# Explicit bounds and skipping in the row gathers of a recommendation kernel on Trainium2

## The chip, the cores and the metric

One core of one Trainium2 chip runs the whole kernel. The engines are named as in the profile: PE (TensorE matmul; PEld is its weight load), DVE (VectorE), ACT (ScalarE), POOL (GpSimd) and SP (SyncE); a trailing "q" (POOLq, SPq) means the engine's sequencer, which reads its instruction list and issues the work. The metric is device time in microseconds (us) of one execution, lower is better. The kernel before takes 32128.78 us, the median of three runs (32128.46 to 32131.62).

## The reference, cut to what matters

A click-through model with an attention over a user's history: 200 history positions (L) for each of 16384 users (B), embeddings of 64 float32 (D), tables of 100000 rows for users and items and 1000 rows for categories. Every history entry is a row fetched from the item table by its index.

```python
u, it, c, h = u_emb[user], i_emb[item], c_emb[cate], i_emb[hist]      # h: [200, 16384, 64]
itb  = broadcast(it, h.shape)
feat = concatenate([h, itb, h - itb, h * itb], axis=-1)
a    = dice(feat @ au_W1 + au_b1, au_alpha, axis=1)   # statistics over the 16384 users
w    = a @ au_W2 + au_b2
cur  = sum(w * h, axis=0)                             # over the 200 positions
z    = concatenate([u, it, c, cur], axis=-1)
z    = dice(z @ W1 + b1, alpha1, axis=0)
z    = dice(z @ W2 + b2, alpha2, axis=0)
out  = z @ W3 + b3
```

All indices given lie inside their tables (0 to 99999 for users and items, 0 to 999 for categories), so no row is ever out of bounds.

## The kernel before, in words

The 16384 users are cut into 128 tiles of 128 users (NT = 128). Sixteen tiles make a chunk, so a history position has 8 chunks (ND = 8, TD = 16). A step k handles one chunk of one position: 200 positions by 8 chunks are 1600 steps. Step k does work of several chunks at once: it fetches the rows of chunk k, transposes and multiplies chunk k - 1 (`turn`, `product`), measures chunk k - 2 (`hidden`, `measure`), and weighs chunk k - 10 into the running sums (`gate`, `weights`, `weigh`, LAG = 10).

Rows come in two ways. `fetch` (line 270) calls `gather` (line 116) once per tile; each call is one indirect DMA issued from POOL, which takes one index per partition out of `idx` and brings 128 rows of 256 bytes into one tile's place in `rows`. `rows` is a ring of five chunk buffers. The chunks 3 and 7 of every position have one tile less to gather (15 instead of 16): the rows of these two tiles are fetched one by one from SP by `rows_by_address` (line 254, its DMAs on line 265) into `side`, and ACT copies them into place. So a position needs 126 gathers, and 200 positions need 25200. Before the loop the same `gather` fetches the item rows (128 calls, line 398, indices from `ids[0]`), and after it the category and user rows (`head_fetch`, line 419, 128 calls each, indices from `ids[1]` and `ids[2]`).

The order on every engine is the order of the code, since all of it stands under a manual schedule; a hardware loop on line 406 runs 4 times over a body of 45 positions (line 408), and the last 20 positions are written out straight (line 441). POOL has nothing to do but gathers, apart from a handful of small instructions at the start. The DMA waits that the framework adds put the gathers on eight completion semaphores in turn, so a gather also waits for the one eight before it to have landed.

Of the kernel before, what the change touches and what calls it, by code (L numbers as in the profile page):

```python
# [32 lines left out]
def din_kernel(  # L33
# [82 lines left out]
    def gather(dst, ids, n, table):  # L116
        nc.gpsimd.indirect_dma_start(  # L117
            out=dst[:, n, :],
            out_offset=None,
            in_=table,  # L120
            in_offset=bass.IndirectOffsetOnAxis(ap=ids, axis=0),
        )

    def load_ids(t, v):
# [145 lines left out]
    def fetch(k):  # L270
        l, c = divmod(k, ND)
        for n in range(TD - has_side(k)):
            j = column(c, n)
            gather(rows[k % ROWS], idx[l % IDX][:, j : j + 1], n, i_emb)
# [98 lines left out]
    with tc.manual_schedule():  # L373
# [20 lines left out]
        for c in range(ND + 1):  # L394
            if c < ND:
                for n in range(TD):
                    j = column(c, n)
                    gather(rows[c % ROWS], ids[0][:, j : j + 1], n, i_emb)
            if c:
                transpose(itT[c - 1], rows[(c - 1) % ROWS])  # L400
# [18 lines left out]
    def head_fetch(k, j):  # L419
        c, u = divmod(j, 2)  # L420
        for n in range(TD):
            i = column(c, n)
            gather(rows[k % ROWS], ids[1 + u][:, i : i + 1], n, (c_emb, u_emb)[u])
# [128 lines left out]
```

## Time and profile before

The profile is of one execution.

| what | value |
|---|---|
| median of three runs | 32128.78 us |
| the profiled execution's own time | 32101.94 us |
| its span, first to last instruction | 32100.2 us |
| gathers from POOL | 25200 in the history steps, 3 x 128 around them |
| rows fetched one by one from SP | 51200 |
| busy share of DVE, the next busiest after POOL and PE | 46% |
| mean granted TensorE clock | 0.719 |

"Busy" counts an engine's own instructions; register, branch, semaphore and DMA-issuing instructions are not in it. "Idle before" is the time that an engine stood still ahead of an instruction, put down to what released it; "issue" as a releaser means that the engine waited for nothing that the profile shows. A line number is that of the instruction in the code above, so all gathers are L117, whichever loop called them.

### The profile page before, as it was taken

Reading aid. Unit: us, or ns where it says so; the run is one execution under the profiler, and the core shown is the slowest. Engines: PE = TensorE matmul, PEld = TensorE weight load, DVE = VectorE, ACT = ScalarE, POOL = GpSimd, SP = SyncE. Lnnn points to the kernel's source line nnn. Section 1 sums busy time; section 2 is a strip of 40 time slices with the busy share of each in tenths; the row PEclk is TensorE's granted clock in tenths of the full one; section 3 lists DMA queues with packets and bytes.
Section 4 is the critical chain, followed back from the end, with each engine's and each line's share of the span. In section 5 each row is a group of like instructions: output and inputs, shape, how many; then the busy total and the mean of one; then the engine's idle time right before and its main releaser. Section 6 shows DMA issues by size and latency. Waiting matters only on the chain. (4 is left out here: it accounts for less than half of the span.)

```text
span 32100.2 us, 224464 instructions
## 1 busy us (share of the span) xinstructions
PE 15661.4 (49%) x26020; PEld 6253.8 (19%) x26020; DVE 14921.9 (46%) x18956; ACT 7823.3 (24%) x7481; POOL 24139.4 (75%) x25589
## 2 busy tenths in 40 slices
PE   4444444444444444444445444454444444445445
PEld 1111121111111111111112111121111211112111
DVE  4444444444444444444444444444444444444443
ACT  2222222222222222222222222222222222222222
POOL 7777777777777777777777777777777777777776
PEclk7777767776777777777777777777777777777777
DMA  1111111111111111111111111111111111111111
GB/s 28 28 28 28 28 28 28 28 27 28 28 28 28 28 28 28 28 27 28 28 28 28 28 28 28 28 28 28 28 28 28 28 28 28 28 28 28 28 28 22
DMA packets 958596, 881.57 MB, mean 27 GB/s; under 512 B 547488, under 2 KB 547688, under 8 KB 957032
## 3 DMA queue, kind: packets, MB, share of 16 engines
q0 software_dynamic: 818688, 839.97, 11.8%
q1 hardware_dynamic: 138056, 27.05, 0.4%
q14 instruction: 1352, 11.08, 0.1%
q8 instruction: 212, 3.47, 0.0%
q10 hardware_dynamic: 288, 0.00, 0.0%
HBM read 865.03 MB, written 0.13 MB: 27 GB/s over the span
## 5 line engine op out<-in xcount | busy, mean ns | idle before, releaser
L117 POOL DMA_INDIRECT rows<-in_L_rec_i_emb,idx x25200 | 23776.6, 944 | 7706.1 <-issue 7132.8
L151 PE MATMUL px<-hT,blk_h 128*128 128x512 f32 x6404 | 5661.5, 983 | 15033.9 <-DVE hT L146 15033.9
L146 DVE STREAM_TRANSPOSE hT<-rows 64x512 f32<-64x512 f32 x6404 | 4519.1, 706 | 12085.3 <-DMA rows<-in_L_rec_i_emb,idx 11421.6
L304 ACT COPY ph<-hT 128x1024 f32<-128x1024 f32 x1601 | 1627.1, 1016 | 18738.7 <-DVE hT L146 18738.7
L151 PEld LDWEIGHTS px<-hT,blk_h 128*128 128x128 f32 x6404 | 1816.6, 314 | 18047.2 <-issue 17233.6
L151 PE MATMUL px<-itT,blk_i 128*128 128x512 f32 x6404 | 4735.4, 832 | 0.0
L151 PE MATMUL wb<-y,blk_w 128*128 128x512 f32 x6440 | 3413.4, 657 | 1245.9 <-DVE y L282 1230.2
L295 DVE BATCH_NORM_STATS2 st<-xs 128x6 f32<-128x512 f32 x3204 | 2058.3, 684 | 3704.4 <-ACT xs L290 3704.4
L151 PE MATMUL px<-hm,blk_m 128*128 128x512 f32 x6408 | 3036.9, 596 | 38.1 <-DVE hm L382 36.4
L290 ACT ACTIVATE xs<-px,au_bias 128x1024 f32<-128x1024 f32 x1602 | 1781.6, 1112 | 4164.1 <-PE px L151 4164.1
L151 PEld LDWEIGHTS px<-itT,blk_i 128*128 128x128 f32 x6404 | 1862.1, 291 | 2859.9 <-issue 2859.9
L282 DVE TENSOR_TENSOR y<-pg,xs 128x1024 f32<-128x1024 f32 x1610 | 1954.9, 1214 | 736.6 <-ACT pg L279 736.4
L286 DVE SCALAR_TENSOR_TENSOR wb<-wb,au_bias,hT 128x1024 f32<-128x1024 f32 x1610 | 2081.1, 1293 | 82.2 <-PE wb L151 30.0
L287 DVE TENSOR_TENSOR curT<-wb,curT 128x1024 f32<-128x1024 f32 x1610 | 1971.2, 1224 | 54.8
L278 ACT ACTIVATE pg<-xs,sh,rs 128x1024 f32<-128x1024 f32 x1610 | 1937.3, 1203 | 79.9 <-DVE sh L387 42.7
L307 DVE TENSOR_TENSOR hm<-ph,itT 128x1024 f32<-128x1024 f32 x1601 | 1942.5, 1213 | 0.0
L279 ACT ACTIVATE pg<-pg,au_al,au_1al 128x1024 f32<-128x1024 f32 x1610 | 1895.1, 1177 | 54.1
L151 PEld LDWEIGHTS wb<-y,blk_w 128*128 128x128 f32 x6440 | 1307.8, 207 | 2976.1 <-issue 1538.0
L151 PEld LDWEIGHTS px<-hm,blk_m 128*128 128x128 f32 x6408 | 1195.9, 191 | 1686.8 <-issue 1236.5
L278 ACT ACT_TABLE_LOAD x206 | 264.3, 1283 | 77.5 <-PEq L406 57.4
L160 ACT ACT_TABLE_LOAD x203 | 260.4, 1283 | 7.5 <-PE pg L461 4.0
L160 ACT ACTIVATE std<-var,eps 128x1 f32<-128x1 f32 x201 | 59.2, 294 | 710.6 <-DVE var L327 710.6
(147 smaller groups left out, 1531.7 us busy)
## 6 DMA issues: line engine op xcount, KB each, us to landing
side<-in_L_rec_i_emb SPq DMA_DIRECT2D x51200, 0.2 KB
rows<-in_L_rec_i_emb,idx POOLq DMA_INDIRECT x25200, 2.4
idx<-in_r_hist SPq DMA_DIRECT2D x200, 63.0 KB
addr<-in_r_hist SPq DMA_DIRECT2D x200, 1.0 KB
rows<-in_L_rec_i_emb,ids POOLq DMA_INDIRECT x128, 2.4
rows<-in_L_rec_c_emb,ids POOLq DMA_INDIRECT x128, 2.3
rows<-in_L_rec_u_emb,ids POOLq DMA_INDIRECT x128, 2.4
w1a<-in_L_rec_W SPq DMA_DIRECT2D x4, 32.0 KB
```

Of the source, the lines that this page charges most:

```text
L117: nc.gpsimd.indirect_dma_start(out=dst[:, n, :], out_offset=None, in_=table, in_offset=bass.IndirectOffsetOnAxis(ap=ids, axis=0),)
L146: nc.vector.transpose(by_tile(dst[ts(e, D)], i), of[ts(i, D), :, ts(e, S)])
L151: nc.tensor.matmul(dst[:, ts(i, CH)], lhsT, rhs[:, ts(i, CH)], start=(first and j == 0), stop=(last and j == len(pairs) - 1), skip_group_c ...
L278: nc.scalar.activation(pg, xs[k % XR], AF.Sigmoid, bias=shifts[i], scale=rstds[i])
L279: nc.scalar.activation(pg, pg, AF.Identity, bias=au_al, scale=au_1al)
L282: nc.vector.tensor_mul(y, pg, xs[k % XR])
L286: nc.vector.scalar_tensor_tensor(wb, wb, au_bias2, hT[k % LAG], ALU.add, ALU.mult)
L287: nc.vector.tensor_add(curT[k % ND], wb, curT[k % ND])
L290: nc.scalar.activation(xs[k % XR], px, AF.Identity, bias=au_bias)
L295: nc.vector.bn_stats(stats[l % 3][:, 2 * c + i, :], xs[k % XR][:, ts(i, CH)])
L304: nc.scalar.copy(ph, hT[k % LAG])
L307: nc.vector.tensor_mul(hm, ph, itT[k % ND])
```

## The change

Both arguments are added to the one call through which all gathers go:

```diff
             in_=table,
             in_offset=bass.IndirectOffsetOnAxis(ap=ids, axis=0),
+            bounds_check=table.shape[0] - 1,
+            oob_is_err=False,
         )
```

With `bounds_check` every index is compared with a bound (99999 for the user and item tables, 999 for the categories), and with `oob_is_err=False` a row whose index is greater is left out and nothing is reported. Without the two arguments the call gives no bound, and the instruction's flag says that an index out of bounds is an error.

In the built program the bound stands in a register of POOL's sequencer. The framework sets it anew ahead of every call: 8574 register moves are added to POOL's list, one ahead of each of the 8574 gathers in it (the loop body's 5670 are run four times). The gather instruction itself then names the register and has the error flag cleared; in the program before, the field of the register is empty and the flag is set. POOL's other instructions, their order and their waits are the same, and so are those of PE, DVE, ACT and SP.

## Prediction

> **What bounds the kernel now.** I read the page first, then the waits, then single instructions. The page's engines and costliest groups:
>
> ```profile
> PE 15661.4 (49%) x26020; PEld 6253.8 (19%) x26020; DVE 14921.9 (46%) x18956; ACT 7823.3 (24%) x7481; POOL 24139.4 (75%) x25589
> POOL 7777777777777777777777777777777777777776
> ...
> L117 POOL DMA_INDIRECT rows<-in_L_rec_i_emb,idx x25200 | 23776.6, 944 | 7706.1 <-issue 7132.8
> ```
>
> POOL looks 75% busy, evenly over the span, but the gather's idle time is not slack: 7706.1 us over 25200 gathers is 306 ns each, nearly all "issue". One gather takes 944 + 306 = 1249 ns from start to start, and 25,584 gathers (25,200 and three times 128) take 25,584 x 1.2493 = 31,962 us of the 32,100.2 us span. A stretch of the timeline confirms that the gap is the same every time (start and duration in us, idle time ahead):
>
> ```profile
> 15011.57 0.94 POOL L117 DMA_INDIRECT rows<-in_L_rec_i_emb,idx  x1 [0.30 <-issue]
> 15012.82 0.94 POOL L117 DMA_INDIRECT rows<-in_L_rec_i_emb,idx  x1 [0.30 <-issue]
> 15014.07 0.95 POOL L117 DMA_INDIRECT rows<-in_L_rec_i_emb,idx  x1 [0.30 <-issue]
> 15015.32 0.94 POOL L117 DMA_INDIRECT rows<-in_L_rec_i_emb,idx  x1 [0.30 <-DMA rows<-in_L_rec_i_emb,idx]
> ```
>
> The waits (in total, times, longest) say whether anyone holds POOL up, and who waits for it:
>
> ```profile
> PE px L151 <- DVE hT L146: 15033.9, 1596, 11.6
> DVE hT L146 <- DMA rows<-in_L_rec_i_emb,idx: 11421.6, 1498, 9.3
> POOL rows L117 <- issue: 7243.4, 23692, 8.0
> POOL rows L117 <- DMA rows<-in_L_rec_i_emb,idx: 533.7, 1750, 0.3
> ```
>
> The last row is no real wait: 533.7 / 1750 = 0.305 us, the ordinary gap. DVE waits 11,422 us for gathered rows, and PE and ACT wait for DVE. SP, the other source of rows, is ahead too: its sequencer stands 10,009 us waiting for DVE. So the pace is POOL's own: whatever a gather gains or loses, times 25,584, is the change of the time. 0.2% of the time, about what a measurement of this kernel can tell from no change, is 64 us or 2.5 ns per gather.
>
> **The register move.** The change adds one to each gather, 25,584 in all. Its price is in the trace, as POOL's sequencer runs one at the loop's entry:
>
> ```profile
> L548 POOLq MOVE  x1: 39/39/39, 153.9 to 153.9; - x1
> ...
> L117 POOL DMA_INDIRECT rows<-in_L_rec_i_emb,ids x128: 940/944/1091, 2.9 to 161.6; - x128
> ```
>
> (durations in ns, then first and last start in us). 39 ns each makes 25,584 x 0.039 = 998 us if none is covered. But the two rows also show cover. That move stands behind the 128 item gathers in the list, and it ran at 153.9 us, when the last of these started at 161.6 us: the sequencer had issued all of them, six gathers ahead of POOL. How fast it can issue shows where it starts anew, at the second pass of the loop:
>
> ```profile
> L117 POOL DMA_INDIRECT rows<-in_L_rec_i_emb,idx x21: 938/944/953, 7249.0 to 7274.0; - x21
> L117 POOLq EVENT_SEMAPHORE  x2: 17/30/43, 7248.2 to 7261.4; - x2
> ```
>
> In the instruction list 16 gathers stand between these two semaphore instructions, so the sequencer issued 16 in 13.2 us, 0.825 us each or less, while POOL started some ten. With a move it is 0.864 us, well under 1.249 us. The 2010 semaphore instructions among the gathers don't lengthen the gap either. I take 0 us; the work that hides it is the gather that POOL is generating. If that cover is gone (if the sequencer may not touch a register while gathers that name it are queued), it is up to 998 us, and DVE's transposes are late by the same. The move has no wait, it passes no other queue, and it can't save time.
>
> More instructions are also read: 25,584 x 64 bytes = 1.6 MB beside the 14.55 MB on the instruction queues, whose share is 0.1%; hidden by the same lead, 0 us.
>
> **The comparison.** A gather now has to take the bound from its register, compare 128 indices and mask rows, as I suppose for what it reads and for what it writes. No row of the trace shows this. What brackets it are POOL's small instructions:
>
> ```profile
> L379 POOL IOTA lanes<- 128x128 int32 x1 | 0.2, 224 | 0.4 <-POOLq L538 0.4
> L538 POOL MEMSET const-uint8-127<- 128x1 uint8 x1 | 0.1, 116 | 0.0
> L538 POOL MEMSET const-float32-0.0<- 128x1 f32 x1 | 0.1, 99 | 0.3 <-issue 0.3
> ```
>
> (mean ns after the comma). One column of 128 values costs (224 - 107) / 127 = 0.92 ns, with 107 ns as the mean of the four MEMSETs (99, 102, 110, 116). It only adds work, so it can't be under nothing. Lower end: the comparison alone, one pass, 0.92 ns, 24 us. Upper end: as much as a whole small POOL instruction with its set-up, 116 ns, 2968 us. Between them I take the bound's fetch at the price of the register move, 39 ns, as the nearest row in which POOL handles one register, and six passes (read index, compare, mask, on each side), 6 x 0.92 = 5.5 ns: 44.5 ns per gather, 25,584 x 0.0445 = 1138 us. It lies in the gather's 944 ns or in the 306 ns behind it; either way it is on the path, since POOL goes from gather to gather without a wait.
>
> [...]
>
> **What is removed** is the error flag. What serving it costs the trace doesn't show. At least 0; at most as much as the comparison, since it too is one test over the rows. I take 0, as without a bound there is nothing to report.
>
> **Moved data.** The bytes stay:
>
> ```profile
> q0 software_dynamic: 818688, 839.97, 11.8%
> ```
>
> 818,688 / 25,584 = 32 packets a gather, at 11.8% of the DMA engines. Landing takes 2.2 to 4.3 us, and only the last gather's is uncovered, as DVE waits for rows all along: a microsecond at most. I take 0.
>
> **The sum.** 32,101.9 (this execution's own time, its span of 32,100.2 and 1.7 us around it) + 0 + 1138 + 0 = 33,240 us. The median of the runs shown is 26.8 us above this execution, so I forecast 33,267 us, 3.5% slower.
>
> **The rivals.**
>
> *The likeliest* (0.58): the comparison is paid in every gather, 2.5 to 116 ns, 32,193 to 35,097 us; 33,267 in it. For it: POOL has no wait in which to hide, and a gather without a bound has nothing to compare. Against it: 944 ns for 128 indices is 7.4 ns each, so much may be fixed work beside which a masked pass is free. An uncovered move alone would give 32,129 + 998 = 33,127 us and would look like this in the total; the gap would tell them apart.
>
> *A dearer path* (0.10): indices are taken one at a time as soon as rows may be skipped. If that adds a quarter of today's 7.4 ns for each index, it is 236 ns, 6038 us, 38,167 us. For it: a skipped row changes how many rows each DMA engine gets, which a fixed layout doesn't allow (the 32 even packets). Against it: nothing in the trace has such a path. It decides from 155 ns on, the 116 ns of the comparison's upper end and 39 ns of uncovered move together.
>
> *Nothing* (0.10): the comparison is made anyway, with a default bound, and only its source changes. 32,129 us, within 64. For it: the flag for an error was set before, which makes sense only if something is tested. Against it: the field of the bound was empty.
>
> *Faster* (0.22): the gather before carries out its test for an error and prepares the report, and clearing the flag takes this work out of POOL's path. Its place is the end of each gather, its price that of the comparison turned round: at 30 ns a gather, 768 us, 31,361 us. It decides as soon as what is saved is over 2.5 ns more than the bound's own price, in which case the time is under 32,065 us. For it: the gap of 306 ns behind each gather has room for such work. Against it: without a bound there is nothing to test against, and the 306 ns stand also behind gathers that wait for nothing.
>
> **How the numbers follow.** Slower is the likeliest and the dearer path, 0.68; same 0.10; faster 0.22. The range ends above where the dearer path begins, 155 ns, 32,129 + 3965 = 36,094 us, which leaves out its 0.10. Below it takes in no change and the faster case up to 15 ns a gather, 384 us, 31,745 us, which leaves out some 0.10 of that case's 0.22. The likeliest case's own range is 32,193 to 35,097 us.
>
> **What would show it.** In the profile after, the gather's mean should read near 944 + 45 ns with the gap at 306 ns; a gap near 345 ns instead means that the register move is not covered, and POOLq should then show no lead at the loop's entry. POOLq must show 25,584 more moves of some 39 ns. PE, DVE and ACT should keep their busy times, and DVE's wait for rows should grow by what POOL loses. A gather that starts later because SP or a landing is late, or a changed number of packets in q0, would prove my picture wrong, and so would a gather below 940 ns.

## The result, and the profile after

The kernel after the change takes 33488.04 us (median of four runs, 33485.28 to 33488.41); the kernel before, run beside it, takes 32129.93 us. The ratio is 1.042 (95% interval 1.040 to 1.044), 1358 us slower. Spread over 25,584 gathers that is 53.1 ns each; the prediction had 44.5 ns and 33,267 us.

The page of the kernel after, its engines, the row of POOL's busy tenths, the gather queue and the gather's group (busy us, mean ns of one, idle before):

```profile
PE 15624.0 (47%) x26020; PEld 6240.6 (19%) x26020; DVE 14943.1 (45%) x18956; ACT 7826.6 (23%) x7481; POOL 25517.3 (76%) x25589
POOL 7777777777777777777777777777777777777776
q0 software_dynamic: 818688, 839.97, 11.3%
q14 instruction: 1551, 12.71, 0.1%
L117 POOL DMA_INDIRECT rows<-in_L_rec_i_emb,idx x25200 | 25133.8, 997 | 7713.3 <-issue 7139.6
```

The gather's mean went from 944 to 997 ns. Its idle time stayed: 7713.3 / 25200 = 306 ns, as before. So what was added lies inside the gather: between the two profiled executions POOL's busy time grew by 1377.9 us (from 24,139.4) and the span by 1386.2 us (from 32,100.2 to 33,486.4). That is 53.9 ns per gather; the medians give 53.1, since the profiled execution of the kernel before was 28 us faster than the median. PE, DVE and ACT have the same work as before, within 0.3%. Packets and bytes of the gathers are the same to the last digit. The instruction queue read 1.63 MB more (12.71 against 11.08), 64 bytes for each added register move.

The same in single instructions, from the timeline of the kernel after (start and duration in us, idle time ahead):

```profile
15011.50 0.99 POOL L117 DMA_INDIRECT rows<-in_L_rec_i_emb,idx  x1 [0.30 <-issue]
15012.80 1.00 POOL L117 DMA_INDIRECT rows<-in_L_rec_i_emb,idx  x1 [0.30 <-issue]
15014.10 1.00 POOL L117 DMA_INDIRECT rows<-in_L_rec_i_emb,idx  x1 [0.30 <-issue]
15015.41 1.00 POOL L117 DMA_INDIRECT rows<-in_L_rec_i_emb,idx  x1 [0.30 <-issue]
```

From start to start it is 1.302 us instead of 1.249, again and again. The register moves are in the trace too. In the view of the gather's line for the whole run, and then for the 45 us from 7555 to 7600, in which the loop's second pass begins, both of the kernel after (durations in ns as min/median/max, first and last start in us):

```profile
L117 POOLq MOVE  x25584: 29/29/39, 0.8 to 33339.7; - x200
L117 POOL DMA_INDIRECT rows<-in_L_rec_i_emb,idx x25200: 992/997/1107, 169.6 to 33015.5; - x199
```

```profile
L117 POOLq MOVE  x36: 29/29/29, 7561.9 to 7599.2; - x36
L117 POOL DMA_INDIRECT rows<-in_L_rec_i_emb,idx x29: 992/997/1007, 7562.8 to 7599.3; - x29
```

All 25,584 are there, at 29 ns. In the second stretch the sequencer has run 36 moves while POOL has started 29 gathers, so it is seven gathers ahead with a move at each: the moves take place while POOL is busy with earlier gathers. Who waits for the gathers pays it all. The waits of the kernel after (in total us, times, longest):

```profile
PE px L153 <- DVE hT L148: 16412.0, 1596, 12.5
DVE hT L148 <- DMA rows<-in_L_rec_i_emb,idx: 12714.8, 1498, 10.2
POOL rows L117 <- issue: 7250.3, 23693, 8.1
```

DVE waits 1293 us longer for gathered rows than before (11,421.6), PE 1378 us longer for DVE; POOL itself still waits for nobody.

### The profile page after: what moved, and what is told of

The parts are those of the page before. It is cut to its first block, busy times and chain, and to the rows that moved or that the text cites. A ratio compares the mean times of both kernels' runs of the same rounds, so it can differ in the third digit from the quotient of the medians.

```text
span 33486.4 us, 250048 instructions
## 1 busy us (share of the span) xinstructions
PE 15624.0 (47%) x26020; PEld 6240.6 (19%) x26020; DVE 14943.1 (45%) x18956; ACT 7826.6 (23%) x7481; POOL 25517.3 (76%) x25589
## 3 DMA queue, kind: packets, MB, share of 16 engines
q0 software_dynamic: 818688, 839.97, 11.3%
q14 instruction: 1551, 12.71, 0.1%
HBM read 865.03 MB, written 0.13 MB: 26 GB/s over the span
## 5 line engine op out<-in xcount | busy, mean ns | idle before, releaser
L117 POOL DMA_INDIRECT rows<-in_L_rec_i_emb,idx x25200 | 25133.8, 997 | 7713.3 <-issue 7139.6
```

The lines of the kernel that those rows point to most:

```text
L117: nc.gpsimd.indirect_dma_start(out=dst[:, n, :], out_offset=None, in_=table, in_offset=bass.IndirectOffsetOnAxis(ap=ids, axis=0), bounds_c ...
```

## The experiments

Three questions are open after the result. Which of the two arguments costs: the bound, or leaving rows out instead of reporting them? Does the cost go by instruction, by index, or by row left out? And do the register moves cost anything in the total? The runs fell on several chips. On two of them the kernel before takes 32,102 and 32,150 us, close to the time above; on two others it takes 46,939 and 46,941 us, and its loop is not paced by POOL there (the last section shows by what). The length of one gather hardly depends on that: it is 944 or 945 ns without a bound on every chip whose trace has such a kernel. So what a part of the change costs is read from the gather's own duration, and the total is used only where POOL sets the pace.

### One argument at a time

The first kernel has the bound and leaves the error flag set, the second only clears the flag.

```diff
+            bounds_check=table.shape[0] - 1,
+            oob_is_err=True,
```

> The bound is given, and an index beyond it is still reported as an error. If the bound's comparison is what costs (my theory), the gather takes 997 ns as with the whole change, the gap stays at 306 ns, and the time is 33,488 us. If leaving rows out is what costs, the gather takes 944 ns and the time is 32,130 us. If reporting errors costs something once there is a bound to test, the gather takes more than 997 ns: every 2.5 ns are 64 us.

```diff
+            oob_is_err=False,
```

> Only the error flag is cleared; no bound, no register move. My theory: 944 ns a gather and 32,130 us, within 64 us. If leaving rows out is what costs: 997 ns and 33,488 us. If serving the error flag costs something in the kernel before (the faster rival of the prediction): under 941 ns a gather and under 32,065 us.

Both ran on the chip where the kernel before takes 46,939 us. The gather's group in the kernel with the bound and the flag:

```profile
L117 POOL DMA_INDIRECT rows<-in_L_rec_i_emb,idx x25200 | 25436.3, 1009 | 21818.4 <-DVE hT L148 13765.1
```

and in the kernel that only clears the flag:

```profile
L117 POOL DMA_INDIRECT rows<-in_L_rec_i_emb,idx x25200 | 23785.7, 944 | 22383.8 <-DVE hT L147 14439.1
```

Clearing the flag alone changes nothing: 944 ns as before, and a total of 46,929.75 us, ratio 0.9999 (0.9989 to 1.0008). The bound alone makes the gather 1009 ns long, 65 ns more than without. With both arguments, as in the change, it is 997 ns (and 996 on this chip, in the next experiment). So the bound is what costs, and once there is a bound, reporting costs another 12 ns, which the change's second argument saves. No row was out of bounds in these runs, so what a report itself costs was not measured. Of the three readings put down for the first kernel, the one with "more than 997 ns" came true. Its total of 48,022.51 us is 1.024 times that of the kernel before (1.022 to 1.026); since POOL stands still for DVE in both (the releaser in the rows), that ratio isn't the gather's price.

### The bound in a register that is set once

```diff
+    bound = {n: nc.gpsimd.to_reg(n - 1) for n in (V, c_emb.shape[0])}
...
+            bounds_check=bound[table.shape[0]],
+            oob_is_err=False,
```

> The whole change, but the bound is put into a register once for each table size, so that 25,582 of the 25,584 register moves are gone. My theory, the moves are covered by the gather before: 997 ns, gap 306 ns, 33,488 us as with them. If the moves cost something: up to 25,584 x 29 ns = 742 us less, 32,746 us. If giving the gather a register at all is what costs, not moving a value into it: 33,488 us too, and this run doesn't tell it from the comparison.

It ran on the same chip as the two above. The gather's row in the view of its line:

```profile
L119 POOL DMA_INDIRECT rows<-in_L_rec_i_emb,idx x25200: 991/997/1052, 169.5 to 48433.3; - x199
```

997 ns without the moves too, so the 53 ns don't come from them. The total was 49,044.78 us, 1.046 (1.044 to 1.047), on a chip where POOL doesn't set the pace. That is more than the 48,022.51 us of the kernel with the bound, the moves and the flag on the same chip, which I can't explain. So this run says nothing about the moves in the total; the last experiment takes that up.

### Fewer rows per gather

Two pairs, each without and with the change. The gather takes only the first 64 (or 16) of its 128 indices; the ring's buffers are zeroed at the start.

```diff
-            out=dst[:, n, :],
+            out=dst[:64, n, :],
...
-            in_offset=bass.IndirectOffsetOnAxis(ap=ids, axis=0),
+            in_offset=bass.IndirectOffsetOnAxis(ap=ids[:64], axis=0),
```

> Every gather without a bound fetches 64 rows instead of 128; the rows of the other 64 users of each tile are left out (they stay at what the buffers held, zeros at first). It is the base for the next kernel. If the gather's 944 ns are mostly fixed: over 800 ns. If they are spent index by index: 472 ns.

> The same with the whole change, so half the rows are left out here too. If the 53 ns are paid index by index or row by row: 26 ns more than the gather of 64 rows without a bound. If they are a fixed price per instruction (the bound's register, the set-up): 53 ns more.

> Every gather without a bound fetches 16 rows; the rows of the other 112 users of each tile are left out. A third point on the line of the gathers without a bound: on a straight line with 128 and 64 rows if the work goes by rows.

> The same 16 rows with the whole change; 112 rows of each tile are left out. Paid by rows: 7 ns more than the gather of 16 rows without a bound. Fixed: 53 ns more.

These four ran on one chip, on which the kernel before takes 32,150 us. The gather's groups, for 64 rows without and with the change, then for 16 rows without and with it:

```profile
L117 POOL DMA_INDIRECT rows<-in_L_rec_i_emb,idx x25200 | 22799.2, 905 | 7717.3 <-issue 7149.1
```

```profile
L117 POOL DMA_INDIRECT rows<-in_L_rec_i_emb,idx x25200 | 23788.0, 944 | 7718.4 <-issue 7146.6
```

```profile
L117 POOL DMA_INDIRECT rows<-in_L_rec_i_emb,idx x25200 | 21359.5, 848 | 7718.0 <-issue 7142.0
```

```profile
L117 POOL DMA_INDIRECT rows<-in_L_rec_i_emb,idx x25200 | 22410.4, 889 | 7717.1 <-issue 7169.3
```

The gap is 306 ns in all four. The totals agree with the means (one run each; the row for 128 is the result above, from four runs each):

| rows per gather | without, us | with the change, us | difference per gather |
|---|---|---|---|
| 16 | 29,702.72 | 30,770.92 | 41.8 ns |
| 64 | 31,166.61 | 32,169.28 | 39.2 ns |
| 128 | 32,129.93 | 33,488.04 | 53.1 ns |

A gather without a bound is mostly fixed: 848 ns for 16 rows, 905 for 64, 944 for 128, where the expectation for a gather paid by rows was 472 ns at 64. The three points don't lie on one straight line either: 57 ns come with the 48 rows from 16 to 64, and 39 ns with the next 64. The price of the bound is mostly fixed too: about 40 ns whether 16 or 64 rows are fetched, and 53 ns for 128. Neither expectation on the bound was quite right. Paid by rows it would have been 7 and 26 ns, wholly fixed it would have been 53 in each pair. Some 40 ns come with the instruction, and some 13 appear between 64 and 128 rows. What the 40 ns are made of these runs don't tell.

### Rows that are really left out

The bound is lowered, so that half of the rows, or 15 of 16, lie beyond it; here too the ring's buffers are zeroed at the start.

```diff
+            bounds_check=table.shape[0] // 2 - 1,
+            oob_is_err=False,
```

> The bound is half the table (49,999 and 499), so about half of the rows are left out and the output is that of zeros or old rows in their places. If masking is done for all rows alike (my theory), the gather still takes 997 ns and the time is 33,488 us within 100 us, while the transferred bytes fall to half. If rows that are left out take a path of their own (the dearer rival), the gather takes longer: a quarter of 7.4 ns for each of 64 rows would be 118 ns more, 3,019 us. If rows left out save their descriptors, it takes less.

> The bound is a sixteenth of the table (6,249 and 61), so about 15 of 16 rows are left out, and the output is that of zeros or old rows in their places. My theory: 997 ns again and a sixteenth of the bytes. Dearer rival: 221 ns more. Descriptors saved: clearly less than at half.

They ran on a chip where the kernel before takes 46,941 us. From the page of the kernel with half the rows, the queue (packets, MB, share) and the gather's group:

```profile
q0 software_dynamic: 818688, 427.21, 6.0%
L117 POOL DMA_INDIRECT rows<-in_L_rec_i_emb,idx x25200 | 25096.7, 996 | 20985.2 <-DVE hT L148 12990.4
```

and of the kernel with one row in 16:

```profile
q0 software_dynamic: 818688, 66.08, 1.5%
L117 POOL DMA_INDIRECT rows<-in_L_rec_i_emb,idx x25200 | 25097.0, 996 | 20866.4 <-DVE hT L148 12851.5
```

The gather takes 996 or 997 ns whether no row, half or nearly all are left out: in the time that the bound adds, no row counts for less because it is left out. The number of packets doesn't change either (818,688). With half the rows gone, 25,584 x 64 x 256 bytes (419.2 MB) and the 16 packets of 4 bytes that each gather has beside its 16 of rows (1.6 MB) would be 420.8 MB; the queue moved 427.2. The rest, 6.4 MB, is 4 bytes for each of 25,584 x 64 rows that are left out (6.5 MB by that count). With 15 of 16 gone the same sum leaves 12.0 MB for 3.07 million rows, 3.9 bytes each. The sizes of the packets settle it. Where nothing is left out, each of the 409,344 packets of rows has 2048 bytes, eight rows (trace of the kernel after). The pages count the packets of all queues by size, first that of the kernel after, then with half the rows, then with one in 16:

```profile
DMA packets 958795, 883.20 MB, mean 26 GB/s; under 512 B 547488, under 2 KB 547688, under 8 KB 957032
```

```profile
DMA packets 958793, 470.42 MB, mean 10 GB/s; under 512 B 561990, under 2 KB 955423, under 8 KB 957032
```

```profile
DMA packets 958793, 109.29 MB, mean 2 GB/s; under 512 B 922164, under 2 KB 957032, under 8 KB 957032
```

If a packet of rows has eight pieces, each of 256 bytes or of 4, it is 32, 284, 536 and so on up to 2048 bytes long. With half the rows gone at random, 9 of 256 such packets are then under 512 bytes and one of 256 is full, which makes 561,879 packets under 512 bytes and 955,433 under 2 KB; with 15 of 16 gone it makes 922,025 and 957,032. The pages have 561,990 and 955,423, and 922,164 and 957,032. So a row left out is replaced with a transfer of 4 bytes rather than dropped, which fits the constant packet count and the constant length of the gather. The pages' "HBM read" stays at 865.03 MB in both kernels, as without a bound, so whether such a row is still read from the table is not shown; the packets did get shorter in time (the queue's share is 6.0% and 1.5%, where the kernel that only clears the flag, on another chip, has 10.2% for as many packets in a span about as long). The totals, 46,879.13 and 46,769.37 us (one run each), were expected at 33,488; that expectation was made for a chip on which POOL sets the pace.

### All rows through POOL, so that POOL's pace decides

To weigh the parts in the total, the last three kernels have no row loads on SP; the rest of their edit, not shown, only makes the code work without them.

```diff
-SIDES = (3, 7)
+SIDES = ()
```

> The kernel before with the two tiles that SP fetched row by row gathered by POOL as well: 25,984 gathers, none with a bound. It takes SP's row loads, which paced the loop on some chips, out of the comparison. If POOL's pace is all that is left: 25,984 x 1.2493 us and the 138 us around them, 32,600 us, whichever chip it runs on. If something else than SP's rows slows those chips: far above 32,600 us there.

> The same with the whole change, the bound in a register that is set once per table size (no move per gather). My theory: 997 ns a gather, gap 306 ns, 25,984 x 53 ns = 1,377 us above the kernel without a bound, 4.2%. If the 25,584 moves of the change had cost something after all: less than that, down to 1,377 - 754 = 623 us above.

> The same with a bound and the error flag left set, and with a register move ahead of every gather. By the 1,009 ns that a gather with bound and flag took before: 65 ns, 1,690 us above the kernel without a bound, 5.2%, with the gap at 306 ns. If the 12 ns over the 997 came of something else on that chip: 1,377 us above. If moves cost something: a gap over 306 ns.

They ran on a chip where the kernel before takes 32,101.94 us.

| kernel, all rows through POOL | median of four, us | ratio to the kernel before |
|---|---|---|
| no bound | 32,588.7 | 1.015 (1.013 to 1.017) |
| bound in a register set once, flag cleared | 33,945.47 | 1.057 (1.056 to 1.059) |
| bound by a move per gather, flag set | 34,300.79 | 1.069 (1.067 to 1.070) |

The view of the gather's line in the first kernel, in the second, which has no move on POOLq there, and in the third, which has one per gather:

```profile
L117 POOL DMA_INDIRECT rows<-in_L_rec_i_emb,idx x25600: 940/945/963, 163.1 to 32176.2; - x199
```

```profile
L119 POOL DMA_INDIRECT rows<-in_L_rec_i_emb,idx x25600: 992/997/1066, 169.9 to 33541.6; - x199
```

```profile
L117 POOLq MOVE  x25984: 29/29/39, 0.8 to 34157.5; - x200
L117 POOL DMA_INDIRECT rows<-in_L_rec_i_emb,idx x25600: 1004/1010/1068, 171.3 to 33830.3; - x199
```

The second kernel is 1356.8 us above the first, 52.2 ns for each of 25,984 gathers, without any moves. The change itself, with its moves, cost 53.1 ns per gather. Four executions of the second kernel lie up to 66 us apart, 2.5 ns per gather, so the moves are free to within some 2 or 3 of their 29 ns. The gap says the same: it is 305 or 306 ns in all three, with and without moves (7818.5 us over 25,600 gathers in the third). The third kernel is 1712 us above the first, 65.9 ns per gather, where 1,690 us were expected; this confirms in the total, on another chip, the 65 ns that bound and flag together cost in the gather's duration. The first kernel was expected at 32,600 us and came to 32,589. Since this chip isn't one of those on which SP's rows are slow, the question that this kernel was also to answer, whether such a chip runs at POOL's pace without them, stays open.

Of the kernels here that fetch every row, none beats the kernel before.

## Why the prediction was right, point by point

**What bounds the kernel**: right. Every nanosecond of a gather came through to the total, 25,584 times (1377.9 us more of POOL's busy time, 1386.2 us more of the span).

**The register move at 0 us**: right. It took 29 ns where the trace of before showed one of 39, was hidden by the gathers that POOL still had to run, and left the gap at 306 ns. (The timeline of before has seven gathers that start after the move at 153.9 us, not six; the reading of the lead holds.) Without the moves the price is the same (52.2 against 53.1 ns). The rival of the uncovered move, 998 us, is refuted, though it would have given a total not far from the forecast. The extra instructions read, 1.63 MB, cost nothing that shows.

**The comparison at 44.5 ns**: right in place and sign, but too small; measured were 53.1 ns, so the forecast missed 220 us of the 1358. The two parts of that sum come out differently. The 39 ns for "the bound's fetch", a fixed price, stand against some 40 ns that are there at 16 rows as at 64. That these are the fetch was not shown, and the price was that of a move in the sequencer, which measured 29 ns in this change (with it the sum would have been 34.5 ns), so the agreement may be luck. The six passes at 0.92 ns, 5.5 ns, are the mis-sized term: at 128 rows 13 ns stand in their place, and between 16 and 64 rows nothing. A column of values in the IOTA row was no measure of a pass inside the gather. The range, 31,745 to 36,094 us, held everything from 15 ns less to 155 ns more per gather, so that the time fell into it says little for these two parts.

**The flag at 0 us**: right in the order in which the prediction took it, since clearing it without a bound changes nothing (0.9999) and the bound then costs 53 ns. In the other order the terms are 65 ns for the bound and 12 to 14 ns back for clearing the flag. The faster rival is refuted for a gather without a bound; where there is one, having the flag set does cost something (1009 against 997 ns).

**The dearer path**: refuted. Rows left out make a gather no longer (996 ns). That a left-out row would upset the layout of the packets was wrong: the 818,688 packets stay, and those of rows get smaller (427.21 and 66.08 MB in all, in place of 839.97).

**Nothing**: refuted, by 53 ns against the 2.5 that can be told.

**Moved data at 0 us**: right, with the same packets and bytes (818,688 and 839.97 MB).

## What to carry to other kernels

When one engine goes from instruction to instruction with a constant gap, count the instructions and look at the price of one: an argument that adds 53 ns to each of 25,584 is worth 4% of this kernel, though it moves no byte and adds no wait. A register move ahead of every such instruction was free here, to within 2 or 3 of its 29 ns, where the sequencer is some seven instructions ahead; a trace shows such a lead where an instruction of the sequencer runs earlier than the work ahead of it in the list (the move at 153.9 us in the prediction, with seven gathers still to start). With every row in range, a gather of 128 rows was cheapest here without a bound (944 against 997 ns); with one, the gather that may skip was cheaper than the one that would report (997 against 1009 ns).

## What the runs showed of the hardware

The kernel before doesn't take the same time on all chips. On two chips it took 46,939 and 46,941 us, 46% more than on the others. The gather is as long there as elsewhere (944 ns), but POOL stands still, as the waits of the kernel that only clears the flag show, taken on one of them:

```profile
POOL rows L117 <- DVE hT L147: 14505.7, 775, 44.7
ACT rows L302 <- DMA side<-in_L_rec_i_emb: 13130.8, 396, 49.5
DVE hT L147 <- ACT rows L302: 8505.2, 396, 39.9
```

Read from the end: ACT waits for the rows that SP loads one by one, DVE for ACT's copy of them, POOL for DVE to free the ring. SP's timeline says how fast these rows go, first a stretch on that chip, then one of the kernel before on the chip of the first profile (start, length in us, number of loads):

```profile
20001.38 137.52 SPq L266 DMA_DIRECT2D side<-in_L_rec_i_emb  x160
```

```profile
15045.82 25.09 SPq L265 DMA_DIRECT2D side<-in_L_rec_i_emb  x64
```

0.86 us a row against 0.39. A position has 256 such rows. At that pace its loads take 220 us of the 235 us that a position takes in all on that chip, and SP waits for hardly anything: no entry among its waits is over 446.4 us in total. On the chip of the first profile, at 0.39 us a row, they take some 100 us of 160, and SP stands 10,009 us waiting for DVE. So on the slow chip SP's loads set the pace. Part of the delay shows in SP's sequencer itself: its register move ahead of a load takes 29 to 38 ns on the first chip, and up to 1435 ns on the other; the load's own instruction takes up to 362 ns on the first and up to 1424 on the other. The medians are the same on both, 29 and 225 ns, so how much of the delay this is was not shown. Why SP's loads go slower on those chips, and why on one of them the kernels with a bound differ by more than their gathers do (1.024 with moves and flag, 1.046 without either), was not tried and stays open.
